# Gated projection in a graph network: two of the seven block products are made by seven products of their own blocks in three quarters of each layer, and the base of the result is kept in memory

## The chip, the cores and the metric

The kernel runs on one core of one Trainium2 chip. The metric is the device time of one execution in microseconds (us). The time before is the median of three runs. A profile of one execution shows what each engine did. The engines are named as in the profile: PE (TensorE, matmuls), PEld (its weight loads), DVE (VectorE), ACT (ScalarE), POOL (GpSimd) and SP (SyncE, which issues most DMAs).

## The reference, cut to what matters

There are 1024 nodes with 512 features, 16384 edges, 16 groups of 64 nodes and 4 layers. All data is float32.

```
h = relu(layernorm(x));  x_in = h
h = gcn(batchnorm(h), gcn_in)
for i in range(4):
    h = h + attention(ln(h, ln2[i]), cond, Wq[i], Wk[i], Wv[i], Wo[i])
    u = ln(h, ln3[i]) @ geglu_w[i] + geglu_b[i]      # 1024x512 @ 512x4096
    val, gate = split(u, 2)                          # 2048 columns each
    h = h + (val * gelu(gate)) @ ffo_w[i] + ffo_b[i] # 1024x2048 @ 2048x512
return x + gcn(h, gcn_out) + x_in
```

The change touches the product that gives `u` (the gated projection), and the sum of `x`, `x_in` and the output bias, which the kernel calls the base of the result.

## The kernel before, in words

**Tiles.** Tiles have 128 partitions. A pool of PSUM tiles has 8 banks (`bank`, 128x512). In SBUF there are 36 large slots (`slot`, 128x2x512), 10 work tiles (`t512`, 128x512) and 6 accumulators (`acc_tile`). The order of the instructions on each engine is fixed when the program is built: a scheduler takes them roughly in the order of the code and puts the semaphore waits in. On the chip each engine works through its own queue in that order.

**Seven products instead of eight.** A large product is cut into 2x2 blocks. `sums_of_a` and `sums_of_b` form sums of the left and right blocks, seven block products are made, and their results are added up. In the gated projection the left blocks are weights: `wval` and `wgate`, each in two halves of the 512 input features. The right blocks are the normalised, turned activations: the two halves of the features by the two halves of the nodes (`ln3T`), with the sums in `ln3S`. The last step of `ln3_sums` runs on POOL (L215), its other steps for the last blocks on DVE (L212 to L214). `geglu_weights` forms the sums of the weights on POOL with four operations over 128x1024 (L219 to L222, tiles `ges` and `wgate`).

**The stage of the gated projection.** A layer has four quarters, r = 0 to 3, of 512 columns of `val` and of `gate` each. A quarter has four quads, c = 0 to 3, of 128 columns. The class `Quad` makes a quad. One block product there (`multiply`, L301) is two matmuls of 128x128 by 128x512, and each shows as two records in the trace, so x4. `first` and `second` make products 0 and 1 into bank `ga`. `rest` makes products 5, 6, 4, 3 and 2:

```
pb:  product 5            u2 = pb + s1       (DVE L939)
pc:  product 6            u3 = pc + u2       (DVE L942)
pd:  product 4            g1 = pd + u3, gelu (DVE L945, ACT L932)
pc:  product 3 on top     g0 = pc + u2, gelu (DVE L949, ACT L932)
pd:  product 2 on top     v1 = pd + bias + u2 (DVE L953)
```

Product 3 accumulates on bank `pc`, so it has to wait until DVE has read product 6 from that bank for `u3`; likewise product 2 waits until DVE has read `pd` for `g1`. `f1 = v1 * g1` (L955) and `f0 = (a + bias) * g0` (L956) are then written to `fT`. `geglu` runs the quads and after each one forms the sums of `fT` for the next product (L975 to L979, on DVE).

**What stands around it.** `ffn_out` multiplies `fT` by a quarter of `ffo_w` (banks `fa` to `fd`) and adds to `h`; in r = 0 to 2 part of these additions runs on POOL (L1006 to L1009). `out_weights` forms the sums of that quarter of `ffo_w`: on DVE in r = 0, beside quad 2, and on POOL in r = 1 to 3 (L212 to L215). At the head of r = 1, POOL adds the bias `ffb` to the eight blocks of `h` (L1279). `geglu_weights` of quarter r + 1 runs on POOL while quarter r is multiplied. In r = 0, the products 0 and 1 of the quads lie among the end of the attention, and the quads begin with `rest`.

**The base.** In quarter r = 3 of the last layer `base_of` loads a block of `x` again, normalises it (L172) and forms `max(xn, 0) + x` (L1270), two blocks for each quad. POOL then adds the output bias (L1316). The eight blocks stay in four slots until the last step `into_out` reads them. `load_last` loads the weights and the graph matrix for the last product.

## Time and profile before

| | |
|---|---|
| median of 3 runs | 2531.46 us (2530.84 to 2531.52) |
| the profiled execution | 2530.76 us; span from first to last instruction 2529.0 us |
| granted TensorE clock | 1.000 |
| busy: PE, PEld, DVE, ACT, POOL | 2507.3, 1768.6, 1400.5, 558.0, 645.1 us |
| as share of the span | 99%, 70%, 55%, 22%, 26% |
| DMA | 156.81 MB, mean 62 GB/s |

Busy time is a union: instructions that overlap on one engine count once. A duration in the tables below is that of one instruction from its start to its end; two that follow each other on DVE or PE overlap somewhat, so that the distance between their starts is the better measure of what each costs. "Idle before" an instruction is the time in which its engine did nothing just before, with what ended it. The records' names leave out buffer numbers.

### The profile page before, as it was taken

To read this page: it belongs to the slowest core of one execution; us is meant where nothing else is said; L and a number is where in the kernel's file an instruction comes from. 1 tells how busy PE (TensorE), PEld (TensorE's weight loads), DVE (VectorE), ACT (ScalarE), POOL (GpSimd) and SP (SyncE) were. 2 spreads that over 40 slices of the span, in tenths; PEclk is the share of its full clock that TensorE was granted. 3 is DMA by queue.
4 is the path that set the end of the run, shared out by engine and by line. 5 is a ranking of instruction groups with operands and counts; after the bars stand their busy time and mean duration, and the time that the engine had idled before them with its cause. 6 is when DMAs were issued, how large, how long until landed. Compare 5 with 4: busy or idle time off the path is not lost. (4 is left out here: it accounts for less than half of the span.)

```text
span 2529.0 us, 32224 instructions
## 1 busy us (share of the span) xinstructions
PE 2507.3 (99%) x12464; PEld 1768.6 (70%) x12464; DVE 1400.5 (55%) x3026; ACT 558.0 (22%) x1318; POOL 645.1 (26%) x539
## 2 busy tenths in 40 slices
PE   8999999999999999999999999999999999999999
PEld 5778886666578887655587888556676888566665
DVE  9655566544574556544484556644474555654461
ACT  7322222111122223111122222211112222211111
POOL 0322224532210003533320003253320002353120
PEclk9999999999999999999999999999999999999999
DMA  6302232111122112010212212110111121111030
GB/s 179 131 32 91 92 127 65 38 51 35 62 61 72 45 61 76 26 54 17 95 36 69 72 63 68 34 54 17 59 67 59 59 71 62 49 34 54 9 100 34
DMA packets 67136, 156.81 MB, mean 62 GB/s; under 512 B 5576, under 2 KB 5904, under 8 KB 66976
## 3 DMA queue, kind: packets, MB, share of 16 engines
q1 hardware_dynamic: 64880, 149.25, 18.1%
q0 software_dynamic: 1376, 4.30, 0.5%
q8 instruction: 103, 1.69, 0.3%
q10 hardware_dynamic: 720, 1.11, 0.1%
q14 instruction: 57, 0.47, 0.1%
HBM read 133.66 MB, written 20.97 MB: 61 GB/s over the span
## 5 line engine op out<-in xcount | busy, mean ns | idle before, releaser
L301 PE MATMUL ga<-ln3T,wval 128*128 128x512 f32 x512 | 233.9, 593 | 0.0
L932 ACT ACTIVATE g<-g,gcols 128x512 f32<-128x512 f32 x128 | 92.4, 722 | 430.3 <-DVE g L945 365.8
L301 PEld LDWEIGHTS ga<-ln3T,wval 128*128 128x128 f32 x512 | 96.0, 190 | 109.9 <-issue 109.1
L776 ACT ACTIVATE pr<-sc,nmax 128x256 f32<-128x256 f32 x256 | 118.2, 475 | 176.8 <-DVE nmax L771 176.8
L847 POOL TENSOR_TENSOR os<-oT 128x256 f32<-128x256 f32 x12 | 8.7, 728 | 566.9 <-DVE oT L822 566.9
L1006 POOL TENSOR_TENSOR hall<-fu,hall 128x512 f32<-128x512 f32 x24 | 30.4, 1268 | 467.1 <-DVE fu L1005 467.1
L301 PE MATMUL pa_v<-wv,ct 128*128 128x256 f32 x512 | 123.1, 379 | 0.0
L301 PE MATMUL fa<-wff,fT 128*128 128x256 f32 x512 | 121.6, 379 | 0.0
L301 PE MATMUL pc_v<-wv,ct 128*128 128x256 f32 x512 | 121.0, 379 | 0.0
L301 PE MATMUL gc<-ln3S,wgate 128*128 128x512 f32 x256 | 120.4, 592 | 0.6 <-DVE gu L942 0.6
L301 PE MATMUL pd_k<-ct,wks 128*128 128x256 f32 x512 | 121.0, 379 | 0.0
L301 PE MATMUL pd_v<-wvs,ct 128*128 128x256 f32 x512 | 120.9, 379 | 0.0
L301 PE MATMUL pc_k<-ct,wk 128*128 128x256 f32 x512 | 120.9, 379 | 0.0
L301 PE MATMUL gd<-ln3T,ges 128*128 128x512 f32 x256 | 120.6, 593 | 0.0
L301 PE MATMUL gb<-ln3S,ges 128*128 128x512 f32 x256 | 120.3, 592 | 0.0
L301 PE MATMUL gc<-ln3T,wgate 128*128 128x512 f32 x256 | 120.3, 592 | 0.0
L301 PE MATMUL gd<-ln3S,ges 128*128 128x512 f32 x256 | 120.3, 592 | 0.0
L301 PE MATMUL pa_k<-ct,wk 128*128 128x256 f32 x480 | 116.2, 385 | 0.0
L301 PEld LDWEIGHTS fa<-wff,fT 128*128 128x128 f32 x512 | 97.3, 190 | 21.8 <-issue 9.6
L301 PEld LDWEIGHTS pd_k<-ct,wks 128*128 128x128 f32 x512 | 97.3, 190 | 13.2
L301 PEld LDWEIGHTS pd_v<-wvs,ct 128*128 128x128 f32 x512 | 97.3, 190 | 13.2
L301 PEld LDWEIGHTS pc_k<-ct,wk 128*128 128x128 f32 x512 | 97.3, 190 | 13.2
(318 smaller groups left out, 4880.9 us busy)
## 6 DMA issues: line engine op xcount, KB each, us to landing
ct<-cond_dram SPq DMA_DIRECT2D x72, 512.0 KB, 4.6
wval<-in_L_gnn_geglu_w_dram SPq DMA_DIRECT2D x32, 512.0 KB, 3.8
wgate<-in_L_gnn_geglu_w_dram SPq DMA_DIRECT2D x32, 512.0 KB, 4.5
wff<-in_L_gnn_ffo_w_dram SPq DMA_DIRECT2D x32, 512.0 KB, 4.5
cond_dram<-ct SPq DMA_DIRECT2D x24, 512.0 KB, 3.1
cond<-in_L_gnn_cond_dram SPq DMA_DIRECT2D x32, 256.0 KB, 4.6
ct<-cond_dram SPq DMA_DIRECT2D x24, 256.0 KB, 4.7
wk<-in_L_gnn_Wk_dram SPq DMA_DIRECT2D x8, 512.0 KB, 5.3
```

What stands on the lines that cost most here:

```text
L301: nc.tensor.matmul(at, left[:, k, l0:l1], right[:, k, r0:r1], start=start and n == 0 and k == 0, stop=n == len(cols_of) - 1 and k == 1, sk ...
L776: nc.scalar.activation(pr3[:, a, :], ps3[:, a, :], AF.Exp, bias=nmax[:, a:a + 1], accum_out=tot[:, a:a + 1])
L847: t.tensor_tensor(s1, a21, a22, OP.add)
L932: nc.scalar.activation(pre, pre, AF.Gelu, bias=gcols[:, cg:cg + 1])
L1006: t.tensor_tensor(h21, halves_of(u2), h21, OP.add)
```

## The change

In quarters 1 to 3 of each layer the quads are run in pairs (c = p and p + 2). Block products 5 and 6 of both quads of a pair are no longer made by two matmuls of 512 columns each for each quad; each is cut into 2x2 blocks again and made by seven matmuls of 128x128 by 128x256 (`Pair.seven`). The sums of the left blocks are formed on POOL (`inner_lefts`, once for each quarter, eight operations over 128x256 into three work tiles and in place), those of the right blocks on DVE (`inner_rights`, once for each layer after quarter 0, eight operations over 128x256 into `wos` and in place). The results are added up on ACT and DVE. Quarter 0 runs its quads as before.

The base of the result is formed in quarter 0 of layers 0 and 1, one block beside each quad, with the output bias added on POOL at once, stored to a DRAM tensor `base_dram`, and loaded again by `load_last`.

```diff
+    base_dram = dram.tile([NB, P, D], F32, name="base_dram")
...
+        def end(self):
+            n, c, bias = self.n, self.c, gcols[:, self.cv:self.cv + 1]
+            pc, pd = bank(f"gc_{n}"), self.d
+            g1 = t512(f"g1_{n}")
+            nc.vector.tensor_tensor(g1, pd, self.u3, OP.add)
+            self.gate(g1, n)
+            self.product(3, pc, True)
+            g0 = t512(f"g0_{n}")
+            nc.vector.tensor_tensor(g0, pc, self.u3, OP.add)
+            self.gate(g0, n)
+            self.product(2, pd, False)
+            nc.vector.scalar_tensor_tensor(self.u2, pd, bias, self.u2, OP.add, OP.add)
+            f0, f1 = (self.fT[i][c // 2][:, c % 2, :] for i in range(2))
+            nc.vector.tensor_tensor(f1, self.u2, g1, OP.mult)
+            self.product(1, self.a, False)
+            nc.vector.scalar_tensor_tensor(f0, self.a, bias, g0, OP.add, OP.mult)
+
+    def inner_left(t, x, s1, s2, s4):
+        blk = [x[:, k, m * M:(m + 1) * M] for m in range(2) for k in range(2)]
+        sums_of_a(t, *blk, s1, s2, s4)
+        return order7(blk, s1, s2, s4)
+    def inner_right(t, y, t1, t2, t4):
+        b11, b12, b21, b22 = (y[:, k, n * M:(n + 1) * M] for k in range(2) for n in range(2))
+        sums_of_b(t, b11, b12, b21, b22, t1, t2, t4)
+        return [b11, b21, b22, t4, t1, t2, b12]
+    INNER = (5, 6)
+    def inner_lefts(l, r, left):
+        rooms = [t512(f"gi_{l}_{r}_{i}") for i in range(3)]
+        rooms = [x[:, i * M:(i + 1) * M] for x in rooms for i in range(2)]
+        return {i: inner_left(nc.gpsimd, left[i], *rooms[3 * n:3 * n + 3])
+                for n, i in enumerate(INNER)}
+    def inner_rights(right):
+        rooms = [wos[:, n, i * M:(i + 1) * M] for n in range(3) for i in range(2)]
+        return {i: inner_right(nc.vector, right[i], *rooms[3 * n:3 * n + 3])
+                for n, i in enumerate(INNER)}
+
+    class Pair:
...
+        def seven(self, i):
...
+            e, f = bank(f"ge_{n}"), bank(f"gf_{n}")
+            a, b, c, d = e[:, :M], e[:, M:], f[:, :M], f[:, M:]
...
+            product(0, a, True)
+            nc.scalar.copy(s1, a)
+            product(5, b, False)
+            nc.vector.tensor_tensor(u2, b, s1, OP.add)
+            product(6, c, True)
+            nc.vector.tensor_tensor(s1, c, u2, OP.add)
+            product(4, d, False)
+            nc.vector.tensor_tensor(to[1][:, M:], d, s1, OP.add)
+            yield
+            product(1, a, False)
+            nc.scalar.copy(to[0][:, :M], a)
+            product(3, c, False)
+            nc.vector.tensor_tensor(to[1][:, :M], c, u2, OP.add)
+            product(2, d, False)
+            nc.vector.tensor_tensor(to[0][:, M:], d, u2, OP.add)
+            yield
+        def run(self, beside):
...
+            q0.product(0, q0.a, True)
+            steps = self.seven(5)
+            next(steps)
+            q1.product(0, q1.a, True)
+            next(steps)
+            for q, w in zip(self.quads, self.w):
+                q.u2 = w
+                nc.vector.tensor_tensor(w, q.a, w, OP.add)
+            steps = self.seven(6)
+            next(steps)
...
+            q0.product(4, q0.d, True)
+            next(steps)
+            for q, w in zip(self.quads, self.w):
+                q.u3 = w
+                nc.vector.tensor_tensor(w, w, q.u2, OP.add)
+            q1.product(4, q1.d, True)
+            for q in self.quads:
+                q.end()
+                beside(q.c)
...
     def load_last():
         w = load_w(gcn_out_w, "w_out")
-        bias = load_row(gcn_out_b, 0, "bias_out")
+        pairs = slots_of(NB // 2, "base")
+        for i, pair in enumerate(pairs):
+            nc.sync.dma_start(pair, base_dram[2 * i:2 * i + 2].rearrange("n p d -> p n d"))
...
         def base_of(nb):
-            if nb + 1 < NB:
+            if nb % 4 < 3:
                 fetch_x(nb + 1)
...
-            nc.vector.scalar_tensor_tensor(base[nb], xn, 0.0, xt, OP.max, OP.add)
+            nc.vector.scalar_tensor_tensor(xn, xn, 0.0, xt, OP.max, OP.add)
+            nc.gpsimd.tensor_tensor(xn, xn, bias_out, OP.add)
+            nc.sync.dma_start(base_dram[nb], xn)
...
             if r:
-                fT, fS, quads = quads_of(l, r, left, right)
...
+                fT, fS, quads = pairs_of(l, r, left, right, (lefts, rights))
             else:
...
+                if l < 2:
+                    if l == 0:
+                        bias_out = load_row(gcn_out_b, 0, "bias_out")
+                    fetch_x(4 * l)
+                def beside(c):
+                    if c == 2:
+                        wff.extend(out_weights(nc.vector, l, 0, raw_out))
+                    if l < 2:
+                        base_of(4 * l + c)
             fT = geglu(quads, fT, fS, not r, beside)
+            if not r:
+                rights = inner_rights(right)
             if r + 1 < R:
                 raw_out = load_out(l, r + 1)
                 left = geglu_weights(l, r + 1, *raw)
+                lefts = inner_lefts(l, r + 1, left)
...
-    for nb in range(NB):
-        nc.gpsimd.tensor_tensor(base[nb], base[nb], bias_out, OP.add)
```

Line numbers of the changed kernel that the prediction uses: the inner sums on DVE and POOL carry L213 to L216 and L220 to L223 (the same helpers, one line lower), the matmuls of `seven` L1021, the `u3` addition L1061, `g1` L964, the bias addition of the base L1389.

More of the change, by code (lines that the diff above doesn't have):

```diff
@@ new lines, in inner_rights, with __init__, product @@
+    def inner_rights(right):
[3 more added lines that the diff above has]
+    class Pair:
+        def __init__(self, l, r, p, left, right, inner, fT):
+            self.n, self.p, self.inner = f"{l}_{r}_{p}", p, inner
+            self.quads = [Quad(l, r, c, left, right, fT) for c in (p, p + 2)]
+        def seven(self, i):
+            n, p = f"{self.n}_{i}", self.p
+            left, right = (x[i] for x in self.inner)
+            e, f = bank(f"ge_{n}"), bank(f"gf_{n}")
+            a, b, c, d = e[:, :M], e[:, M:], f[:, :M], f[:, M:]
+            t = acc_tile(f"gt_{n}")
+            to = self.w = [acc_tile(f"gw{q}_{n}") for q in range(2)]
+            s1, u2 = t[:, :M], t[:, M:]
+            def product(k, to, start):
+                nc.tensor.matmul(to, left[k][:, p * P:(p + 1) * P], right[k], start=start,
+                                 stop=True, skip_group_check=True)
+            product(0, a, True)
[15 more added lines that the diff above has]
+        def run(self, beside):
+            q0, q1 = self.quads
+            for q in self.quads:
+                q.a = bank(f"ga_{q.n}")
+            q0.product(0, q0.a, True)
[8 more added lines that the diff above has]
+            next(steps)
+            for q in self.quads:
+                q.d = bank(f"gd_{q.n}")
+            q0.product(4, q0.d, True)
[4 more added lines that the diff above has]
+            q1.product(4, q1.d, True)
+            for q in self.quads:
+                q.end()
+                beside(q.c)
@@ L958, in quads_of, with pairs_of @@
+    def pairs_of(l, r, left, right, inner):
+        fT = [slots_of(2, f"fT_{l}_{r}_{i}") for i in range(2)]
+        return (fT, slots_of(3, f"fs_{l}_{r}"),
+                [Pair(l, r, p, left, right, inner, fT) for p in range(2)])
     def quads_of(l, r, left, right):
@@ L962, in geglu, with sums @@
     def geglu(quads, fT, s, begun, beside=lambda c: None):
-        for c, q in enumerate(quads):
-            if not begun:
-                q.first()
-            last = q.rest()
-            if not begun:
-                q.second()
-            last()
+        def sums(c):
             k = c % 2
-            beside(c)
             a11, a12, a21, a22 = (fT[i][j][:, k, :] for i in range(2) for j in range(2))
@@ L979, in geglu @@
                 nc.vector.tensor_tensor(s4, a12, s2, OP.subtract)
+        for c, q in enumerate(quads):
+            if begun:
+                q.rest()()
+                beside(c)
+                sums(c)
+            else:
+                q.run(sums)
         return order7([*fT[0], *fT[1]], *s)
@@ L1131, in load_last @@
             nc.gpsimd.dma_start(again[d].bitcast(F32R).rearrange("p a b -> p (a b)"), c_dram[d])
-        return w, bias
+        return w, [pairs[nb // 2][:, nb % 2, :] for nb in range(NB)]
     wks_0 = weight_sums(raw_wk, "wks_0")
@@ L1256, in gnn_kernel @@
         lnT = None
-        base, fetched = [], {}
+        fetched = {}
         def fetch_x(nb):
@@ L1281, in gnn_kernel @@
                 raw = load_geglu(l, r + 1)
+            beside = lambda c: None
             if r:
-                fT, fS, quads = quads_of(l, r, left, right)
-                beside = lambda c: None
-                if last and r == R - 1:
-                    beside = lambda c: [base_of(2 * c + i) for i in range(2)]
-            else:
-                if last:
-                    base.extend(rows_of("base"))
-                    fetch_x(0)
+                fT, fS, quads = pairs_of(l, r, left, right, (lefts, rights))
+            else:
                 wff = []
-                beside = lambda c: wff.extend(
-                    out_weights(nc.vector, l, 0, raw_out) if c == 2 else [])
+                if l < 2:
[7 more added lines that the diff above has]
+                        base_of(4 * l + c)
             fT = geglu(quads, fT, fS, not r, beside)
+            if not r:
+                rights = inner_rights(right)
             if r + 1 < R:
@@ L1302, in gnn_kernel @@
                 if last:
-                    w_out, bias_out = load_last()
+                    w_out, base = load_last()
                 else:
```

## The prediction

> **What bounds the kernel now.** I first read the head of the page.

> ```profile
> span 2529.0 us, 32224 instructions
> PE 2507.3 (99%) x12464; PEld 1768.6 (70%) x12464; DVE 1400.5 (55%) x3026; ACT 558.0 (22%) x1318; POOL 645.1 (26%) x539
> ```

> PE is busy nearly always, so an us saved or lost on PE is an us of the result. Whether its busy time is dense, the timeline of PE over quarter 0 of layer 0 and the product after it tells (start, duration, engine, line, tiles, count):

> ```profile
> 429.31 1.88 PE L301 MATMUL gb<-ln3S,ges 128*128 128x512 f32 x4
> 431.02 1.88 PE L301 MATMUL gc<-ln3T,wgate 128*128 128x512 f32 x4
> 432.74 1.88 PE L301 MATMUL gd<-ln3S,ges 128*128 128x512 f32 x4
> 434.45 1.88 PE L301 MATMUL gc<-ln3S,wgate 128*128 128x512 f32 x4
> ...
> 460.64 1.88 PE L301 MATMUL gc<-ln3S,wgate 128*128 128x512 f32 x4
> ...
> 470.60 1.89 PE L301 MATMUL fa<-wff,fT 128*128 128x256 f32 x8
> 472.33 1.89 PE L301 MATMUL fc<-wffs,fT 128*128 128x256 f32 x8
> ```

> Four records of 512 columns take 1.717 us from start to start (429 ns each), eight of 256 columns 1.73 us (216 ns). No gap stands between groups. So half the columns cost half the time, and PE has no slack to give.

> Then I asked what DVE and POOL do when both work, because the change puts sums on both. This is quarter 1 of layer 0, POOL first, DVE after it:

> ```profile
> 498.50 2.36 POOL L221 TENSOR_TENSOR ges<-ges,wval 128x1024 f32<-128x1024 f32 x1
> 500.94 2.68 POOL L222 TENSOR_TENSOR ges<-wval,ges 128x1024 f32<-128x1024 f32 x1
> 503.58 1.72 POOL L212 TENSOR_TENSOR wffs<-wff 128x512 f32<-128x512 f32 x1
> ```

> ```profile
> 499.23 2.18 DVE L955 TENSOR_TENSOR fT<-gv,g 128x512 f32<-128x512 f32 x1
> 501.33 0.74 DVE L956 SCALAR_TENSOR_TENSOR fT<-ga,gcols,g 128x512 f32<-128x512 f32 x1
> 502.10 2.07 DVE L975 TENSOR_TENSOR fT<-fT,fT 128x512 f32<-128x512 f32 x1
> 504.09 0.68 DVE L939 TENSOR_TENSOR gu<-gb,gs 128x512 f32<-128x512 f32 x1
> ```

> L955 has all its operands in SBUF. It takes 2.18 us instead of the usual 0.69 and ends at 501.41, 0.55 after POOL's L221 (500.86). POOL's next operation in its turn is 0.32 longer than the 2.36 of its sisters. L975 waits in the same way for L222. L956 and L939 read a PSUM bank and run at full pace beside POOL. So a DVE operation with SBUF operands alone and a POOL operation exclude each other, and they take turns. [...]

> Last, where POOL's long operations stand in quarter 0, and what DVE does there:

> ```profile
> 429.61 2.36 POOL L219 TENSOR_TENSOR ges<-wgate,wgate 128x1024 f32<-128x1024 f32 x1
> 432.05 2.35 POOL L220 TENSOR_TENSOR wgate<-wval,wgate 128x1024 f32<-128x1024 f32 x1
> 434.35 2.37 POOL L221 TENSOR_TENSOR ges<-ges,wval 128x1024 f32<-128x1024 f32 x1
> 436.80 2.35 POOL L222 TENSOR_TENSOR ges<-wval,ges 128x1024 f32<-128x1024 f32 x1
> ```

> ```profile
> 431.22 0.69 DVE L939 TENSOR_TENSOR gu<-gb,gs 128x512 f32<-128x512 f32 x1 [2.37 <-PE gb L301]
> 432.94 0.69 DVE L942 TENSOR_TENSOR gu<-gc,gu 128x512 f32<-128x512 f32 x1 [1.02 <-PE gc L301]
> 453.54 0.69 DVE L949 TENSOR_TENSOR g<-gc,gu 128x512 f32<-128x512 f32 x1 [1.02 <-PE gc L301]
> ```

> The weight sums run from 429.61 to 439.15, right beside the first quad (in layer 1 from 1015.17, 0.32 after its `gb`). DVE has only PSUM work there and 1 to 2 us of idle before each, so today nothing collides.

> **The gain on PE.** Product 5 of two quads is 8 records of 429 ns, 3.43 us. Seven narrow matmuls are 14 records of 216 ns, 3.02 us. That saves 0.41 us; two products, two pairs, 12 quarters make 48 times, **19.8 us**. [...]

> **Loss A: the inner sums of the right blocks (layers 2 and 3).** In the order of the changed program six of the eight DVE sums into `wos` stand directly ahead of `u2` of quad 0 (L940), and on POOL the four weight sums still stand right behind the last step of `ln3_sums`. All six have SBUF operands alone, so they take turns with POOL: two pass before POOL's first long operation, then one at each boundary, and the sixth waits for the fourth. POOL's own end is 439.15; add 0.2 for a late start and 0.2 at each of three boundaries (half of the 0.32 to 0.45 that a 512-wide DVE operation costs it): 439.95. The sixth sum starts 0.14 before that record's end (as L955 did) and takes 0.33, `u2` 0.60, `u3` 0.69: 441.4. PE wants to put product 3 on bank `gc` at 434.45 and waits for `u3` to have read it. Queued behind it is all of PE. The stall is 7.0 us (6.3 if the sums cost POOL nothing; 7.6 if 0.4 each). Twice: **14.0 us**.

> **Loss B: the base beside quarter 0 (layers 0 and 1).** Here POOL's bias additions for c = 0, 1, 2 stand ahead of the weight sums in POOL's queue, each waiting for DVE's `base_of`. So the inner sums pass freely at the start, but the weight sums are held up and start only after the third addition. DVE makes g0 of c = 2 at 453.54 to 454.14; L172 and the maximum take 1.26 (0.54 and 0.69 in the last layer before), the addition 1.27, so the weight sums start at about 456.9. Ahead of `u3` of quad 3 DVE then has five SBUF-only operations: one inner sum in place (behind the bias addition), f1, and three of `out_weights`; the last of them waits for the fourth weight sum. Four times 2.36 and four turns of 0.3: 467.5; the last 0.6 and `u3` 0.69: 468.7. PE wants bank `gc` at 460.64, so it stalls 8.0 us (7 to 9.4). Twice: **16.0 us**.

> **Loss C and D: smaller collisions.** C: after quarter 0 of layers 0 and 1 the sums of `fT` on DVE take turns with the fourth bias addition and the 128x256 inner sums on POOL (0.73 each, from L874); `fd` waits for those sums. I take two POOL operations less the cover, 1.5 us, twice: 3.0 (0 to 6). D: in a pair, DVE has after the last matmul of `seven` two additions (0.43, 0.33), two `u3` additions (0.60 each, SBUF only) and `g1` (0.69), 2.65 us, before PE may put product 2 on `gd`. PE's cover is product 3 and half of product 1, 1.72 + 0.86 = 2.58. That is even, but where POOL has long operations each `u3` addition is held up for what is left of 2.36. The first pair of quarter 1 always meets the weight sums: most of one and of a second, less slack elsewhere, 1.7 us, four times; quarter 2 half overlaps, 0.5, four times; the rest 0.1, sixteen times. That is 10.4, say **10 us** (no pair held: 0; eight pairs held twice at 1.75: 28). No reason allows a gain here.

> **Edits at nothing.** The ten extra DVE additions of a pair (0.33 each, 3.3 us) fit: DVE would have some 14 us of work in 23.2 us of PE. POOL's eight inner sums (5.8 us for each quarter) fit into the 26 us idle before L1006 at 471.64; without that cover PE would wait for them. Moving `base_of` out of the last quarter takes away the two short PE waits of that quarter (`gc` 0.6 and `fd` 0.5 us, both on DVE, after 2400 us): **1.1 us** saved. The 2 MB that `load_last` loads are wanted only by the last step, some 60 us later; on SP's queue the stores of the base hold back the load of `wff` for quarter 1 until about 457, and it is wanted some 60 us later.

> **The sum.** −19.8 − 1.1 + 14.0 + 16.0 + 3.0 + 10 = +22.1 us. The profiled execution took 2530.76 us, 0.70 below the median, so **2553 us**. What a measurement of this kernel can tell from no change is about 0.2%, 5 us.

> **The rivals.** *Faster.* If DVE, once it has the turn, keeps it for its whole queue, the six sums take 6 x 0.33 = 2.0 us and `u3` is done before 434.45: A is 0, B is one POOL operation instead of four, about 1 each, C and D some 4. That gives about −15 us, 2516. It decides once A to D together stay under 20.9. For it: at 718.26 one 0.16 us DVE operation slipped in behind another between two POOL operations. Against it: at 2440.80 and 2442.37 (L978, L979) two consecutive DVE sums each waited for a POOL operation, 1.64 and 1.75 us. Chance 0.15.

> *One collision missing.* If the weights of quarter 1 land late, POOL's sums move away from the six and A is 0: +8 us, 2539. Before, no such wait shows at L219. It lies in the range.

> *Dearer.* Each matmul of `seven` waits for a read of its own bank by ACT or DVE. If about 1 us of each `seven` is bare, 48 times, the result is near 2600. Against it: the same chain in the attention (`wab`, `wcd`, 897.59 to 902.77) runs dense at 0.86 for four records, with two banks and other work between, and the changed order puts wide matmuls between the narrow ones. Chance 0.08, with 0.01 in it for narrow records that are dearer than the rows say.

> **How the numbers follow.** My forecast has 0.72 (2536 with A and B at their low ends and C and D at 0; 2571 with A to C high and D at 21); 0.05 lie within 0.2%, losses that just eat the gain. The range 2530 to 2575 leaves out the faster case and little more. Faster 0.15, same 0.05, slower 0.80.

> **What would show it.** Right: in quarter 0 PE idles about 7 us before `gc` of quad 0 in layers 2 and 3 and about 8 us before `gc` of quad 3 in layers 0 and 1, both put down to DVE's `gu`; DVE's rows for `wos` and `wffs` there take 2 to 3 us each; `gd` in the first pair of quarter 1 waits 1 to 2 us for `g`; the narrow matmuls of L1021 stand 216 ns apart. Wrong: PE dense through quarter 0 (then 2516), or gaps inside every `seven` (then 2600).

## The result and the profile after

The changed kernel takes 2566.52 us (median of 4 runs, 2565.66 to 2567.06) against 2531.49 us for the kernel before on the same chip: ratio 1.0138, 95% interval 1.0121 to 1.0156. It is 35 us slower. The prediction had the sign, and 2566.52 lies in its range, but 2553 was 13.5 us too low.

The head of the page of the changed kernel (its profiled execution took 2566.26 us; the mean granted clock is 0.993, before it was 1.000):

```profile
span 2564.5 us, 33202 instructions
PE 2502.6 (98%) x12752; PEld 1821.7 (71%) x12752; DVE 1548.8 (60%) x3298; ACT 560.8 (22%) x1366; POOL 730.9 (29%) x635
```

PE's idle time grew from 21.7 to 61.9 us. PE's busy time fell by 4.7 us only, where 19.8 were expected. So two things are to be found: idle time, and busy time that should have gone. What PE waited for (us in total, times, longest) names the idle time:

```profile
PE gc L302 <- DVE gu L943: 15.1, 2, 7.5
PE gc L302 <- POOL gi L220: 14.1, 2, 7.2
PE gd L302 <- DVE g L964: 8.0, 8, 1.8
PE fd L302 <- DVE fs L1085: 2.2, 2, 1.1
PE ge L1021 <- DVE gt L1027: 1.6, 4, 0.6
```

The first row is loss B (layers 0 and 1, quad 3), the second loss A (layers 2 and 3, quad 0), the fourth C, the third and fifth D. The releaser of the second row reads POOL, but the DVE timeline shows the way: in layer 2, `u3` (L943) stands behind six inner sums, and the last four of these take 2.56 us instead of 0.42. First DVE, then POOL:

```profile
1622.99 2.57 DVE L215 TENSOR_TENSOR wos<-ln3T,wos 128x256 f32<-128x256 f32 x1
...
1630.45 2.56 DVE L216 TENSOR_TENSOR wos<-ln3S,wos 128x256 f32<-128x256 f32 x1
...
1634.06 0.69 DVE L943 TENSOR_TENSOR gu<-gc,gu 128x512 f32<-128x512 f32 x1 [0.46 <-DVE gu L940]
```

```profile
1622.75 2.53 POOL L220 TENSOR_TENSOR ges<-wgate,wgate 128x1024 f32<-128x1024 f32 x1
...
1630.32 2.40 POOL L223 TENSOR_TENSOR ges<-wval,ges 128x1024 f32<-128x1024 f32 x1
```

The first two rows shown end at 1625.56 and 1633.01, POOL's first and last at 1625.28 and 1632.72: one DVE operation passes at each boundary of POOL's. These are the turns that the prediction worked with. Loss B has the same form. In layer 0, POOL's weight sums start at 457.67, behind the third bias addition, and `u3` of quad 3 stands behind five SBUF-only operations on DVE, four of them 2.2 to 2.8 us long. The last one ends just behind POOL's fourth weight sum. DVE first, then POOL:

```profile
466.18 2.82 DVE L215 TENSOR_TENSOR wffs<-wff,wffs 128x512 f32<-128x512 f32 x1
468.93 0.68 DVE L943 TENSOR_TENSOR gu<-gc,gu 128x512 f32<-128x512 f32 x1
```

```profile
465.79 2.66 POOL L223 TENSOR_TENSOR ges<-wval,ges 128x1024 f32<-128x1024 f32 x1
```

Most of the busy time that did not go is in the timeline of PE behind the stalls. In layer 0:

```profile
461.10 1.03 PE L302 MATMUL fa<-wff,fT 128*128 128x256 f32 x4
469.66 3.78 PE L302 MATMUL gc<-ln3S,wgate 128*128 128x512 f32 x4 [7.53 <-DVE gu L943]
473.23 2.90 PE L302 MATMUL gd<-ln3T,ges 128*128 128x512 f32 x4
475.97 1.03 PE L302 MATMUL fa<-wff,fT 128*128 128x256 f32 x4
```

From start to start the four records of `gc` take 3.57 us and those of `gd` 2.74, where 1.717 is usual: 2.88 us more. Two rows of the table of one-us windows around it give the reason (the window's length, busy us of PE, PEld, DVE, ACT and POOL with their instructions, the granted clock, then DMA; the clock is 1.00 in the rows ahead of the first and 0.50 in those between):

```profile
465.00:466.00 1.00, 0.00 (x0) 0.00 (x0) 1.00 (x1) 0.00 (x0) 0.92 (x2) 0.52 0.00 0
...
475.00:476.00 1.00, 1.00 (x4) 0.50 (x3) 0.00 (x0) 0.00 (x0) 0.00 (x0) 0.86 0.00 0
```

The clock fell to 0.50 at 465.04 (0.04 us of that window at full clock, the rest at half), while PE waited, and rose only at 475.28, 5.6 us after PE had gone on. The clock falls in the same way in each of the four long stalls, and after none of the waits of up to 1.8 us in the gated projection. The extra time of the two groups behind the stall is 2.88, 1.50, 2.25 and 2.98 us in layers 0 to 3, together **9.6 us**.

### The profile page after: what moved, and what is told of

It reads as the page before. It is cut to its first block, busy times and chain, and to the rows that moved or that the text cites. A ratio compares the mean times of both kernels' runs of the same rounds, so it can differ in the third digit from the quotient of the medians.

```text
span 2564.5 us, 33202 instructions
## 1 busy us (share of the span) xinstructions
PE 2502.6 (98%) x12752; PEld 1821.7 (71%) x12752; DVE 1548.8 (60%) x3298; ACT 560.8 (22%) x1366; POOL 730.9 (29%) x635
## 3 DMA queue, kind: packets, MB, share of 16 engines
q8 instruction: 105, 1.72, 0.3%
## 5 line engine op out<-in xcount | busy, mean ns | idle before, releaser
L302 PE MATMUL ga<-ln3T,wval 128*128 128x512 f32 x512 | 245.6, 593 | 0.0
L933 ACT ACTIVATE g<-g,gcols 128x512 f32<-128x512 f32 x128 | 87.1, 716 | 375.1 <-DVE g L946 144.9
L302 PE MATMUL gc<-ln3S,wgate 128*128 128x512 f32 x256 | 127.4, 622 | 29.1 <-DVE gu L943 15.1
L302 PE MATMUL gd<-ln3S,ges 128*128 128x512 f32 x256 | 128.1, 592 | 0.0
L302 PEld LDWEIGHTS gc<-ln3S,wgate 128*128 128x128 f32 x256 | 50.1, 198 | 82.1 <-issue 47.2
L302 PEld LDWEIGHTS pa_v<-wv,ct 128*128 128x128 f32 x512 | 97.1, 190 | 13.5 <-issue 0.4
```

The lines of the kernel that those rows point to most:

```text
L302: nc.tensor.matmul(at, left[:, k, l0:l1], right[:, k, r0:r1], start=start and n == 0 and k == 0, stop=n == len(cols_of) - 1 and k == 1, sk ...
L933: nc.scalar.activation(pre, pre, AF.Gelu, bias=gcols[:, cg:cg + 1])
```

## The experiments

The theory: DVE and POOL take turns on SBUF-only operations, PE stalls for that, and each long stall brings a stretch at half clock. The rivals: the base alone, or the inner sums for themselves, are the cause; or the slow stretches have another cause than the stalls. The first four expectations put 2.9 us, layer 0's figure, on each slow stretch; the four measured ones came later.

### The weight sums wait for the inner sums

POOL's weight sums of quarter 1 wait until DVE has done the six early inner sums. No instruction changes its place on any engine.

```diff
-        sums_of_b(t, b11, b12, b21, b22, t1, t2, t4)
+        inner_right.last = sums_of_b(t, b11, b12, b21, b22, t1, t2, t4)
...
-                left = geglu_weights(l, r + 1, *raw)
+                with nullcontext() if r else waiting_for(inner_right.last,
+                                                         mybir.EngineType.Pool):
+                    left = geglu_weights(l, r + 1, *raw)
```

> Only POOL's four weight sums of quarter 1 now wait for the last of the six early inner sums on DVE; the queues keep their order. Theory (turns of DVE and POOL, and a granted clock of half after each long stall): in layers 2 and 3 the six sums run at 0.33 us each, the stall of 7.2 us at gc of quad 0 goes, and so does the slow stretch behind it (2.9 us): 2 x (7.2 + 2.9) = -20 us, 2546. In layers 0 and 1 nothing changes (7.5 us at gc of quad 3, clock 0.5 behind it). Rival 1, the turns are not the cause and the six sums are long for themselves: the weight sums start later and the time does not fall, 2566 or a few us more. Rival 2, the slow stretches come from something else than the stalls: -14 us, 2552, with clock 0.5 still there in layers 2 and 3.

Measured: 2548.69 us (2547.79 to 2549.5), ratio to before 1.0068 [1.0054, 1.0082], 17.8 us less than the changed kernel, where 20 were expected. The DVE timeline of layer 2 now has the sums at their own length, and `u3` begins 3.6 us after `gb` instead of 11.7:

```profile
1623.85 0.41 DVE L215 TENSOR_TENSOR wos<-ln3T,wos 128x256 f32<-128x256 f32 x1
...
1624.85 0.41 DVE L216 TENSOR_TENSOR wos<-ln3S,wos 128x256 f32<-128x256 f32 x1
...
1626.81 0.69 DVE L943 TENSOR_TENSOR gu<-gc,gu 128x512 f32<-128x512 f32 x1 [0.94 <-PE gc L302]
```

In layers 2 and 3 the stall at `gc` of quad 0 is gone, only a wait of 0.6 us at `gc` of quad 1 stands there, and the clock stays at 1.00; in layers 0 and 1 both stay (7.5 us and half clock). The six sums cost nothing by themselves. Loss A is POOL's turns, shown.

### The base as before

`base_of` goes back to the last quarter of the last layer, and the bias addition to the end.

```diff
-            if nb % 4 < 3:
+            if nb + 1 < NB:
                 fetch_x(nb + 1)
...
-            nc.vector.scalar_tensor_tensor(xn, xn, 0.0, xt, OP.max, OP.add)
-            nc.gpsimd.tensor_tensor(xn, xn, bias_out, OP.add)
-            nc.sync.dma_start(base_dram[nb], xn)
+            nc.vector.scalar_tensor_tensor(base[nb], xn, 0.0, xt, OP.max, OP.add)
...
+                if last and r == R - 1:
+                    blocks = iter(range(NB))
+                    beside = lambda c: [base_of(next(blocks)) for _ in range(2)]
...
-                    if l < 2:
-                        base_of(4 * l + c)
```

> The base is formed in the last quarter of the last layer again, as before the change; the pairs and inner sums stay. Theory: without POOL's bias additions the weight sums of layers 0 and 1 start at the head of quarter 0, so these two layers now get the stall of layers 2 and 3 (7.2 us at gc of quad 0, clock 0.5 behind it) in place of 7.5 at gc of quad 3; the waits at fd (1.1 each) go, the two short waits of the last quarter (1.1 together) come back. 2 x (7.2 - 7.5) - 2.2 + 1.1 = -1.7 us, about 2565. Rival, the base is what costs layers 0 and 1 their stall: 2 x (7.5 + 2.9 + 1.1) less 1.1 = -22 us, 2545.

Measured: 2560.32 us (2559.53 to 2561.53), ratio 1.0117 [1.0102, 1.0133], 6.2 us less than the changed kernel; the theory said 1.7, the rival 22. The stalls moved as the theory says; what PE waits for shows that all four layers now have the one at quad 0:

```profile
PE gc L301 <- POOL gi L219: 27.4, 4, 6.9
```

Of the 4.5 us between 1.7 and 6.2, shorter waits give 2.3 (`gc` 27.4 instead of 29.2, `gd` 7.1 instead of 8.0, `fd` 0.9 instead of 2.2, less the 1.7 that the theory had) and the slow matmuls behind the stalls 0.5 (9.1 instead of 9.6); the rest is not settled. Taking the base away doesn't free layers 0 and 1, because the weight sums then come early and meet the inner sums there too.

### Both together

> The two edits before together: base as before the change, weight sums behind the inner sums. Theory: no long stall is left in any layer, and no slow stretch: 2 x (7.2 + 2.9) + 2 x (7.5 + 2.9 + 1.1) - 1.1 = -42 us, 2524, below the time before the change; that is 20 us more than the two edits give one by one, because either alone leaves layers 0 and 1 a stall. What is left of the loss are the waits in pairs (about 9 us). Rival, each edit works for itself: the sum of the two single results. Rival, each matmul of seven waits: still above 2531.

Measured: 2526.64 us (2525.82 to 2528.59, 11 runs), ratio 0.9983 [0.9974, 0.9992]: 39.9 us less than the changed kernel, while the two edits alone give 17.8 + 6.2 = 24.0. The expected 42 had four slow stretches at 2.9 us; with the measured 9.6 us in their place it is 40. No clock window in quarter 0 is below 1.00, and the waits at `gc` sum to 2.5 us in four. That either edit alone leaves two long stalls, and both together none, is what the theory asks for; the rival of independent effects is out. What is left of D (`gd` 7.1 us) is the largest new wait.

### The stalls filled with matmuls

In the quads with a long stall, product 4 is made five times into the same bank.

```diff
-            self.product(4, pd, True)
+            for _ in range(1 + self.again):
+                self.product(4, pd, True)
```

> As the changed kernel, but in the quads with the long stall (quad 3 of quarter 0 in layers 0 and 1, quad 0 in layers 2 and 3) product 4 is made five times into the same bank instead of once, so that PE works through 6.9 us of the stall; the data are the same, and nothing later waits longer. Theory (PE's own idleness lowers the granted clock): the clock stays at 1 behind the four places, 4 x 2.9 = -11.5 us, 2555, although PE is busy 27 us more. Rival, the slow matmuls behind the stall come from something else, such as DVE and POOL at work in SBUF: clock 0.5 there as before, 2566.

Measured: 2568.00 us (2567.59 to 2569.14), no gain: a miss, for a reason of the experiment. In layers 2 and 3 it did what it should: the filled stall ends without a wait, and the clock is 1.00. But in layers 0 and 1 the longer product 4 made the scheduler put `g1` (L948) further back on DVE, behind five SBUF-only sums instead of two, and a new stall of 5.6 us stands at `gd`, with half clock behind it (0.54 from 475 to 480). So it was repeated for layers 2 and 3 alone, where the order on DVE stays:

> As the changed kernel, but only in layers 2 and 3, where the order on DVE stays as it is, product 4 of quad 0 is made five times into the same bank (6.9 us of matmuls, the same data). Theory (PE's idleness lowers the granted clock): the stall of 7 us turns into matmuls of the same length, and the slow stretch behind it (2.25 us in layer 2, 2.98 in layer 3) goes: -5.2 us, 2561, with 27.5/2 us more of busy PE. Rival, the slow matmuls have another cause: 2566.5, no change.

Measured: 2561.66 us (2561.11 to 2562.07), 4.9 us less than the changed kernel, expected 5.2. The timeline of PE in layer 2:

```profile
1625.67 8.75 PE L302 MATMUL gd<-ln3S,ges 128*128 128x512 f32 x20
1634.78 1.95 PE L302 MATMUL gc<-ln3S,wgate 128*128 128x512 f32 x4 [0.36 <-issue]
1636.57 1.88 PE L302 MATMUL gd<-ln3T,ges 128*128 128x512 f32 x4
```

`gc` begins at 1634.78, against 1634.85 in the changed kernel, so the wait for DVE is as long as ever; but the groups behind it stand 1.79 and 1.72 us apart instead of 3.55 and 2.13. PE did 13.7 us more work and the kernel got faster. DVE and POOL did the same work in both. The granted clock is 1.00 from 1620 to 1640 us and from 2210 to 2240, where in the changed kernel it falls to 0.50. That PE's own idleness lowers the clock is shown.

### The base alone

The kernel before with only the second half of the change (its diff is the base's part of the change above).

> The kernel before with only the second half of the change: the base formed in quarter 0 of layers 0 and 1 and kept in memory; no pairs, no inner sums. Theory (POOL's weight sums, held back behind the bias additions, take turns with the sums on DVE): layers 0 and 1 get the stall at gc of quad 3 without any inner sum, shorter by about one POOL operation since DVE has one sum less there: 5 to 7 us each, the clock at half behind it (1.5 to 2.9 us), 0.7 to 1.1 at fd, less the 0.75 that the last quarter gains: +13 to +21 us, about 2548. Rival, it takes the inner sums to make the stall: within 2 us of the time before, 2531.

Measured: 2547.07 us (2545.95 to 2547.37), ratio 1.0062 [1.0048, 1.0075], 15.7 us more than before, where 13 to 21 were expected. What PE waits for, and the first weight sum on POOL in layer 0:

```profile
PE gc L302 <- DVE gu L943: 11.0, 2, 5.5
```

```profile
456.92 2.80 POOL L220 TENSOR_TENSOR ges<-wgate,wgate 128x1024 f32<-128x1024 f32 x1
```

The weight sums start behind the third bias addition, at 456.92 instead of 429.61, and meet `out_weights` on DVE. Loss B needs no inner sum; it is the base's. With the pairs it is 7.5 instead of 5.5 us.

### The stalls cut short

Product 4 of quad 0 repeated twice in layer 2 and once in layer 3.

> As the changed kernel, with product 4 of quad 0 repeated twice in layer 2 and once in layer 3, so that PE is left idle for about 3.8 us there and 5.1 us here. In the four long stalls the clock fell 2.9 to 4.8 us after the last matmul: so 5.1 us should lower it (and cost some 2 us), 3.8 lies within the span and may go either way; where it does not fall, the matmuls behind stand at 429 ns a record at once. Rival, a stall's cost goes by its length alone: both cheaper in proportion.

Measured: 2564.88 us (a single run). The expectation's 2.9 to 4.8 us from the last matmul to the fall should read 2.5 to 4.8, since in layer 3 it is 2.47. Both shortened stalls still cost a slow stretch:

```profile
1634.29 3.75 PE L302 MATMUL gc<-ln3S,wgate 128*128 128x512 f32 x4 [3.79 <-POOL gi L220]
1637.84 2.94 PE L302 MATMUL gd<-ln3T,ges 128*128 128x512 f32 x4
...
2227.40 3.47 PE L302 MATMUL gc<-ln3S,wgate 128*128 128x512 f32 x4 [5.14 <-POOL gi L220]
2230.71 1.88 PE L302 MATMUL gd<-ln3T,ges 128*128 128x512 f32 x4
```

Up to the next group they cost (1640.61 − 1634.29) − 3.43 = 2.9 us after 3.79 us of idleness, and (2232.42 − 2227.40) − 3.43 = 1.6 us after 5.14. The shorter stall costs more. So the price doesn't go by the stall's length, and the rival expectation falls; the last section shows what it went by here.

### Product 1 ahead of product 2

Both edits, and in the first quad of each pair:

```diff
             f0, f1 = (self.fT[i][c // 2][:, c % 2, :] for i in range(2))
+            if c < 2:
+                self.product(1, self.a, False)
+                nc.vector.scalar_tensor_tensor(f0, self.a, bias, g0, OP.add, OP.mult)
             self.product(2, pd, False)
             nc.vector.scalar_tensor_tensor(self.u2, pd, bias, self.u2, OP.add, OP.add)
             nc.vector.tensor_tensor(f1, self.u2, g1, OP.mult)
-            self.product(1, self.a, False)
-            nc.vector.scalar_tensor_tensor(f0, self.a, bias, g0, OP.add, OP.mult)
+            if c >= 2:
+                self.product(1, self.a, False)
+                nc.vector.scalar_tensor_tensor(f0, self.a, bias, g0, OP.add, OP.mult)
```

> The base as before the change and the weight sums behind the inner sums (2526.6 us), and besides in the first quad of each pair product 1 is made ahead of product 2. Theory (the waits at gd in pairs are a want of cover: DVE has 2.65 us to do and POOL holds up the u3 additions): 1.72 us of cover more take 7.1 us of waits down to about 2: 2521.5. Rival, f1 then comes later and the wait goes to the sums behind it (ge of the next pair, fd): no change, 2526.6.

Measured: 2519.46 us (2518.78 to 2520.53), ratio 0.9953 [0.9939, 0.9966]: 12 us faster than the kernel before, 47 faster than the changed one. The waits at `gd` are down from 7.1 to

```profile
PE gd L301 <- DVE g L963: 2.3, 4, 0.6
```

So D was a want of cover, and 1.72 us more of it on PE pay for most of it. The gain over both edits together is 7.2 us, where 5.1 were expected; 4.8 of them are the waits at `gd`, and a wait of 1.2 us at `gf` gave way to one of 0.5 at `ge`.

## Why the prediction was right, and where its sum was short

The sizes below are from start to start of the matmul groups, less what they take without a wait.

- **The gain on PE** (19.8): right. `fa` of quarter 3 follows `fa` of quarter 2 after 70.59 us instead of 72.24, 1.65 less, which is 4 x 0.41; the records of L1021 stand 216 ns apart.
- **Loss A** (14.0): 7.38 + 7.02 = 14.4. **Loss B** (16.0): twice 7.70, 15.4, with the weight sums starting at 457.67 (forecast 456.9). **C** (3.0): 2.5, the two waits at `fd`. The way of each was as written: the `wos` and `wffs` rows of 2 to 3 us, the idle time ahead of `gc` of quad 0 and of quad 3.
- **D** (10): 13.8. It is read from the time from the `fa` of one quarter to that of the next. With the gain of 1.65 us added back and B, C and the slow matmuls taken off, quarter 1 is longer than before by 3.5 us in layers 0 and 1 and by 1.8 in layers 2 and 3, quarter 2 by 0.75 in each layer, quarter 3 by nothing. As idle time it shows only 9.6 us, in 12 waits. `gd` in the first pair of quarter 1 waits up to 1.8 us for `g`, as said.
- **The last quarter** (1.1 saved): 1.6. The wait at `gc` stood ahead of its `fa` and had made the quarter 0.86 us longer than its sisters; the wait at `fd` stood behind it, and from `fa` to the first matmul of the last product it is now 27.67 us instead of 28.42.
- **The term that failed: the price of a stall.** The sum took a stall of 7 us for 7 us. Behind each, matmuls ran at half speed and cost 1.5 to 3.0 us more, 9.6 us in all, and the fill in layers 2 and 3 shows that this is the stall's doing. Nothing in the trace of before could show it there: the clock was 1.000 and no wait of PE in the gated projection was over 0.6 us. Stalls of 7 and 8 us were forecast in the text, but the prediction has no estimate of what PE's records cost behind them. (It takes no stall of that length: a wait of 2.32 us was enough once, as the last section shows.) That 2566.52 still lies in the range is owed to the room left there for dearer losses A to D, not to a term for the clock.
- **The rest of the 13.5 us:** 0.9 us is a slow stretch at 86 to 90 us, ahead of all that the change touches, and not its doing; it is in the traces of the changed kernel, the base as before and both fills. The weight sums behind the inner sums and product 1 ahead of product 2 have one at 27 to 30 us instead, and the other traces have none. Losses A to D came out 3.1 us above their forecast (46.1 against 43.0), most of it D, and the last quarter saved 0.5 us more than forecast. 0.3 us more lies in the last product. Between the profiled executions, which are 35.5 us apart, that leaves nothing over.
- **The rivals.** *Faster* fell: DVE did not keep the turn, and the four sums stood 2.48 to 2.49 us from start to start, one to each POOL operation. *Dearer* fell: the waits inside `seven` are 1.6 us in all. *One collision missing* did not happen. Where the experiment took loss A away, the time fell by 17.8 us, more than the 14 that this rival counted, because the slow matmuls behind the stalls went too.

## What to carry to other kernels

Before work is put on an idle engine, look at which long operations of its neighbour it will stand beside: four sums of 0.33 us cost 7 us here because each waited for one POOL operation of 2.4 us, and one wait that lets the short ones go first gave 18 us back. Price a stall of PE at its length plus the half-clock stretch behind it: here such a stretch came with every stall of 3.79 us and more in the gated projection (1.5 to 3.0 us lost by each in the changed kernel) and with one wait of 2.32 us ahead of it, and with none of the waits of up to 1.8 us in the gated projection. And undo two suspects together as well as singly: the base and the inner sums hid behind each other, and the edits gave 24 us one by one and 40 together.

## What the runs showed of the hardware that was not expected

By this reading a stall need not be long; what counts is how it lies in the grid. The early fall agrees. This wait of 2.32 us is in the changed kernel (first row) and in the one with the weight sums behind the inner sums (second row):

```profile
85.13 2.75 PE L302 MATMUL pa_kT<-ct,wk 128*128 128x256 f32 x8 [2.32 <-DVE v_deg L134]
...
86.23 1.97 PE L302 MATMUL pa_kT<-ct,wk 128*128 128x256 f32 x8 [2.32 <-DVE v_deg L134]
```

In the first it runs from 82.81 to 85.13, inside the one window from 82.75 to 86.16, and the clock falls at that window's end. In the second it runs from 83.91 to 86.23 and lies across two windows (their border is at 84.98), in which PE is busy for 65 and 58%, and the clock stays at 1.00.

What a stall cost depended on the grid too. In the changed kernel PE worked at a clock of 0.50 from its return to the rise, for 5.62, 2.84, 4.38 and 5.85 us in layers 0 to 3, and the groups behind the stall took 2.88, 1.50, 2.25 and 2.98 us more, about half of that. The rise came each time at the end of the first window that PE filled to 83% or more. After the shorter of the two cut stalls PE came back in the middle of a window (at 1634.29, the window ended at 1636.54), and the clock rose at the end of the next one, at 1639.95; after the longer it came back 0.36 us into a window, and the clock rose at its end, at 2230.46. By these edges PE worked at half clock for 5.66 us after the stall of 3.79 us and for 3.06 us after the one of 5.14, which is why the shorter cost more.
